# Layer 1's queries at the border between the layers: eighteen tiles as nine pairs in seven quadrant products, and the last block's two tiles beside its keys

## The chip, the cores and the metric

The kernel runs on one core of a Trainium2 chip. The metric is the device time of one execution in microseconds. Five engines take part, each with its own in-order stream of instructions: PE (TensorE, matrix products), DVE (VectorE), ACT (ScalarE), POOL (GpSimd) and SP (SyncE, which here only issues transfers). ACT and POOL issue transfers too, and an issue stands in its engine's stream like any other instruction.

## The reference

Two layers of a graph transformer over 2,708 tokens of width 512, with eight heads of width 64, a feed-forward of width 2,048, and a sparse adjacency (about 3 entries in 1,000):

```python
mask = adj.astype(jnp.float32) + jnp.eye(n, dtype=jnp.float32)
q = (h @ Wq.T + bq).reshape(n, N_HEADS, D_K)
k = (h @ Wk.T + bk).reshape(n, N_HEADS, D_K)
v = (h @ Wv.T + bv).reshape(n, N_HEADS, D_K)
scores = jnp.einsum('nhd,mhd->hnm', q, k) / jnp.sqrt(jnp.float32(D_K))
scores = jnp.where(mask[None, :, :] == 0, jnp.float32(-1000000000.0), scores)
attn = jax.nn.softmax(scores, axis=-1)
ctx = jnp.einsum('hnm,mhd->nhd', attn, v).reshape(n, D_MODEL)
attn_out = ctx @ Wo.T + bo
h1 = _layer_norm(h + attn_out, ln1_g, ln1_b)
ff = jax.nn.relu(h1 @ W1.T + b1) @ W2.T + b2
h2 = _layer_norm(h1 + ff, ln2_g, ln2_b)
```

The output of layer 0 is the input of layer 1. All arithmetic is in float32.

## The kernel before

The tokens are 22 tiles of 128, the last of 20. The neighbours of each token are found first, as lists. Attention then works tile by tile on gathered rows: for each chunk of neighbours POOL gathers one row of keys and values per token (L1119, `kv_d` to `kv`), DVE multiplies the keys with the tile's queries and sums by head (L1156, L1162), ACT takes the exponential and weighs the values (L1175, L1182), and DVE adds them up (L1195). A tile ends with DVE's reciprocal (L1218) and eight scalings on ACT (`cx`, L1226). PE has no part in that; it does the projections and the feed-forward.

The feed-forward takes two tiles at a time, a block. The eleven blocks run in the order (20,19), (18,17), (8,9), (7,10), (6,11), (5,12), (4,13), (3,14), (2,15), (1,16), (21,0), and `order` is that list laid flat. `blocks[0]` of layer 1 is thus (20,19), and the last block of layer 0 is (21,0). A block has 16 steps `f`, after each of which `advance(credit)` draws a few attention steps from the generator `attend`, for the tiles of the next block; `until(g)` draws until tile `g` is attended. In most blocks the two tiles are multiplied by `W1` and `W2` in quadrants, seven products for eight (the *forms* are the sums and differences of the weights' quadrants that this needs; DVE makes them with `form_apart`, L1694 to L1697, and they are stored in `form_d`).

The order of the work is written out by hand. Each engine executes its instructions in the order in which the code writes them, so a line that is written earlier stands earlier in each queue that it uses, and an instruction that waits holds up what is written behind it on its engine. Buffers come from pools with a fixed number for each tag: `row` has 3 (queries before their store, residuals `xb`), `kv` 5 (the gathers' ring), `acc` 2, `cx` 3, `cT` 3, `h` 4, `hT` 1. A write to such a buffer waits until the last use of its former content has ended, a store included.

Between the layers, in the stage called the border here:

- After each block of layer 0, `keys_values` turns the two tiles (`zT`), computes their layer 1 keys and values on PE, and stores them. It also stores `zT` in `zT_d`. For the last block (21,0) this stands behind everything else, because layer 1's attention can begin only when all keys are there.
- `query(g, zT)` computes one tile's queries: four products of 128x512 on PE (L626), one DVE row from PSUM that scales by 1/8 and adds the bias (L1468, the *eviction*), and a store to `q_d`, which is issued one tile later (`kept`, L1479).
- Two tiles' queries lie beside the last keys, fourteen beside the first attention steps, and four around the first two attended tiles, 20 and 19. The two of block (21,0) are computed in block 0's feed-forward of layer 1 (`asking`), and later blocks ask nothing more. Their `zT` come back from `zT_d`: eight loaded in the last block of layer 0 (`preloaded`, in the places of `acc`, `cx` and `h`), two with `two` (in `hT`), the others with `queries` (in `cT`).
- When tile 20 and tile 19 are attended, `attended` turns them, projects them (`o`), adds the residual and normalises: DVE makes the variance (`va`, L1279), POOL its inverse root (`rd`, L1281), DVE scales. `turned` then turns the result, and block 0 begins (L1596).

Of the kernel before, what the change touches and what calls it, by code (L numbers as in the profile page):

```python
# [18 lines left out]
P = 128  # L19
# [21 lines left out]
KVB = 5  # L41
# [446 lines left out]
def by_edges(ctx: ExitStack, tc: tile.TileContext, x, xT, adj, layers, out, redo):  # L488
# [144 lines left out]
    def plus_rest(to, o, r, scale=None):  # L633
        for part in rest(o, r):
            if scale is None:
                nc.vector.tensor_tensor(to, part, to, ALU.add)
            else:
                nc.vector.scalar_tensor_tensor(to, part, scale, to, ALU.mult, ALU.add)

# [718 lines left out]
    class Layer:  # L1358
        def __init__(self, n, w):
            self.n, self.w, self.w1, self.w2, self.due = n, w, [], [], None  # L1360
            self.stages = []
            self.apart, self.other = True, False
# [65 lines left out]
        def preloaded(self, tiles, temp):  # L1428

            places = []  # L1430
            for _ in range(2):
                both = at.tile([P, SLOTS, DM], F32, tag="acc", name="zTs", bufs=2)
                places += [both[:, i] for i in range(SLOTS)]
            places += [at.tile([P, DM], F32, tag="cx", name="zTs", bufs=CXB) for _ in range(CXB)]
            places.append(temp())
            places = [place.rearrange("p (c t) -> p c t", c=NC) for place in places]
            for g, place in zip(tiles, places):
                nc.sync.dma_start(out=place, in_=zT_d[self.n][g])
            return list(zip(tiles, places))

        def two(self, tiles):

            both = dn.tile([P, 2, NC, P], F32, tag="hT", name="zTs", bufs=1)
            for i, g in enumerate(tiles):
                nc.sync.dma_start(out=both[:, i], in_=zT_d[self.n][g])
            return both

        def queries(self, tiles):

            zTs = []  # L1450
            for i in range(len(tiles) + 1):
                while len(zTs) < min(i + 3, len(tiles)):
                    zT = dn.tile([P, NC, P], F32, tag="cT", name="zT", bufs=3)
                    nc.sync.dma_start(out=zT, in_=zT_d[self.n][tiles[len(zTs)]])
                    zTs.append(zT)
                yield
                if i < len(tiles):
                    self.query(tiles[i], zTs[i])
            self.kept()
            yield  # L1460

        def query(self, g, zT):
# [3 lines left out]
            q = project(lambda c: zT[:, c, :r], r, self.wq, "q", self.other and self.apart)  # L1466
# [788 lines left out]
```

## Time and profile before

| | |
|---|---|
| median of 3 runs | 1817.35 us (1817.26 to 1817.72) |
| profiled execution, its own time | 1817.08 us |
| its span | 1815.1 us |
| PE busy | 1791.5 us (99%) |
| DVE busy | 1463.3 us (81%) |
| ACT busy | 1001.1 us (55%) |
| POOL busy | 855.4 us (47%) |
| last keys of layer 1 beside two queries | 1052.4 to 1070.6 us |
| fourteen queries beside the first attention steps | 1070.6 to 1121.3 us |
| first two attended tiles and four queries | 1121.3 to 1143.7 us |
| block 0's feed-forward, up to the next block's second projection | 1143.7 to 1185.4 us |

Times in the trace count from the span's start. A row of a timeline gives the start, the busy time, the engine, the line and the operation, with "output<-input" by the program's names; "x8" means that eight like instructions are drawn together, and a bracket names what the engine waited for before it. A row of waits gives the waiting instruction, what released it, the sum in microseconds, the number of waits and the longest. A row of the groups by line ends with the busy time and the mean of one instruction in nanoseconds. A row of the transfers ends with the median time from issue to landing. A row of the windows gives the stretch, its length, then for PE, PE's weight loads, DVE, ACT and POOL the busy time and the number of instructions, then the granted clock, the busy share of the DMA engines and GB/s.

### The profile page before, as it was taken

Reading aid. Unit: us, or ns where it says so; the run is one execution under the profiler, and the core shown is the slowest. Engines: PE = TensorE matmul, PEld = TensorE weight load, DVE = VectorE, ACT = ScalarE, POOL = GpSimd, SP = SyncE. Lnnn points to the kernel's source line nnn. Section 1 sums busy time; section 2 is a strip of 40 time slices with the busy share of each in tenths; the row PEclk is TensorE's granted clock in tenths of the full one; section 3 lists DMA queues with packets and bytes.
Section 4 is the critical chain, followed back from the end, with each engine's and each line's share of the span. In section 5 each row is a group of like instructions: output and inputs, shape, how many; then the busy total and the mean of one; then the engine's idle time right before and its main releaser. Section 6 shows DMA issues by size and latency. Waiting matters only on the chain. (4 is left out here: it accounts for less than half of the span.)

```text
span 1815.1 us, 23887 instructions
## 1 busy us (share of the span) xinstructions
PE 1791.5 (99%) x6839; PEld 1214.6 (67%) x6839; DVE 1463.3 (81%) x2599; ACT 1001.1 (55%) x3397; POOL 855.4 (47%) x830
## 2 busy tenths in 40 slices
PE   9999999999999999999999999999999999999997
PEld 4444456666777867777677644666666888788786
DVE  4987778988989889799896267988888899989933
ACT  5771436645555555555653104677776677767631
POOL 3333755534454544454540132556665665655312
PEclk9999999999999999999999999999999999999999
DMA  9997987757676675666752777967867787877531
GB/s 335 369 344 252 374 284 245 230 181 241 203 238 220 203 259 192 208 220 202 241 194 73 242 285 272 319 193 256 279 186 263 243 264 237 293 225 234 173 94 36
DMA packets 186728, 426.74 MB, mean 235 GB/s; under 512 B 20550, under 2 KB 83898, under 8 KB 186584
## 3 DMA queue, kind: packets, MB, share of 16 engines
q0 software_dynamic: 76992, 264.49, 44.0%
q1 hardware_dynamic: 99434, 139.01, 22.5%
q10 hardware_dynamic: 10158, 21.61, 3.1%
q8 instruction: 56, 0.92, 0.2%
q14 instruction: 88, 0.72, 0.1%
HBM read 357.13 MB, written 57.11 MB: 228 GB/s over the span
## 5 line engine op out<-in xcount | busy, mean ns | idle before, releaser
L1119 POOL DMA_INDIRECT kv<-kv_d,listed x420 | 526.0, 1252 | 307.2 <-DVE acc L1195 145.8
L1780 PE MATMUL pf<-hT,w 128*128 128x256 f32 x1792 | 407.2, 379 | 2.1 <-ACT ft L1791 2.1
L1780 PEld LDWEIGHTS pf<-hT,w 128*128 128x128 f32 x1792 | 339.2, 190 | 59.2 <-issue 11.0
L1182 ACT ACTIVATE kv<-kv,p 128x64 f32<-128x64 f32 x1232 | 311.0, 335 | 5.0
L1156 DVE TENSOR_TENSOR kv<-kv,q 128x1024 f32<-128x1024 f32 (+1 forms) x222 | 257.1, 1158 | 14.1 <-DMA q<-q_d,ident_i 10.9
L1162 DVE TENSOR_REDUCE sc<-kv 128x16 f32<-128x1024 f32 (+1 forms) x222 | 258.0, 1162 | 7.6
L1195 DVE TENSOR_TENSOR acc<-acc,kv 128x1024 f32<-128x1024 f32 (+2 forms) x178 | 205.6, 1155 | 49.6 <-ACT kv L1182 36.9
L1596 PEld LDWEIGHTS pf<-hT,w 128*128 128x128 f32 x1024 | 178.5, 190 | 55.3 <-issue 34.6
L1596 PE MATMUL pf<-hT,w 128*128 128x256 f32 (+1 forms) x1024 | 214.6, 357 | 0.1
L1791 ACT ACTIVATE ft<-pf,b 128x256 f32<-128x256 f32 x168 | 78.1, 466 | 214.1 <-PE pf L1780 211.4
L1569 PE MATMUL a<-w,ft 128*128 128x512 f32 x416 | 194.6, 592 | 0.0
L1175 ACT ACTIVATE p<-sc,listed 128x8 f32<-128x8 f32 x420 | 103.6, 295 | 127.9 <-DVE sc L1162 116.5
L1281 POOL TENSOR_TENSOR rd<-va,mhalf 128x1 f32<-128x1 f32 (+1 forms) x48 | 43.8, 913 | 230.8 <-DVE va L1279 230.7
L626 PE MATMUL o<-wo,cT 128*128 128x512 f32 x336 | 151.0, 593 | 0.3 <-ACT cT L1354 0.3
L1188 DVE TENSOR_TENSOR kv<-kv,p 128x512 f32<-128x512 f32 (+1 forms) x178 | 123.6, 694 | 4.8 <-ACT p L1175 4.5
L1569 PEld LDWEIGHTS a<-w,ft 128*128 128x128 f32 x416 | 77.7, 190 | 57.5 <-issue 52.0
L626 PEld LDWEIGHTS o<-wo,cT 128*128 128x128 f32 x336 | 63.4, 190 | 69.3 <-issue 59.6
L1331 POOL TENSOR_SCALAR va<-sq 128x1 f32<-128x1 f32 (+1 forms) x40 | 17.2, 429 | 188.4 <-ACT xb L1324 101.9
L751 DVE MAX8 tops<-code 128x8 f32<-128x247 f32 (+2 forms) x242 | 78.8, 400 | 28.0 <-ACT code L746 27.9
L1226 ACT ACTIVATE cx<-acc,su 128x64 f32<-128x64 f32 (+1 forms) x352 | 88.2, 333 | 11.2 <-DVE su L1218 6.2
L1182 ACT ACTIVATE acc<-kv,p 128x64 f32<-128x64 f32 (+1 forms) x352 | 88.8, 335 | 1.4
L746 ACT ACTIVATE code<-aj 128x1354 bf16<-128x1354 int32 (+1 forms) x44 | 73.5, 1724 | 23.7 <-POOL aj L740 19.0
(258 smaller groups left out, 2793.8 us busy)
## 6 DMA issues: line engine op xcount, KB each, us to landing
forms<-form_d SPq DMA_DIRECT2D x294, 128.0 KB, 3.8
aj<-in_adj SPq DMA_DIRECT2D x42, 677.0 KB, 6.3
kv_d<-kvs ACTq DMA_DIRECT2D x21, 512.0 KB, 7.4
h<-ln_b POOLq DMA_DIRECT2D x41, 256.0 KB, 7.0
xg<-in_xT SPq DMA_DIRECT2D x19, 512.0 KB, 8.0
w<-in_W SPq DMA_DIRECT2D x16, 512.0 KB, 6.4
kv<-kv_d,listed POOLq DMA_INDIRECT x420, 6.5
zT_d<-zT SPq DMA_DIRECT2D x22, 256.0 KB, 5.3
```

Source lines behind the costliest of these rows:

```text
L626: nc.tensor.matmul(o[:r], xs(c), wm[:, c, :], start=(c == 0), stop=(c == NC - 1))
L1119: return nc.gpsimd.indirect_dma_start(out=to, out_offset=None, in_=table[:, :], in_offset=bass.IndirectOffsetOnAxis(ap=s, axis=0), bounds_ ...
L1156: nc.vector.tensor_tensor(kv[:r, :c, :DM], kv[:r, :c, :DM], self.q[:r].unsqueeze(1).to_broadcast([r, c, DM]), ALU.mult,)
L1162: nc.vector.tensor_reduce(self.sc[:r, s0 : s0 + c, :], kv[:r, :c, :DM].rearrange("p s (h d) -> p s h d", d=DK), AX.X, ALU.add,)
L1175: nc.scalar.activation(p[:r, s, :], self.sc[:r, s, :], AF.Exp, bias=minus[:r, g, s : s + 1])
L1182: nc.scalar.activation(to[:, i, hd], kv[:r, i, DM + h * DK : DM + (h + 1) * DK], AF.Copy, scale=p[:r, s0 + i, h : h + 1],)
L1188: nc.vector.tensor_tensor(to[:, 0, :].rearrange("p (h d) -> p h d", d=DK), kv[:r, 0, DM:].rearrange("p (h d) -> p h d", d=DK), p[:r, s0, : ...
L1195: nc.vector.tensor_tensor(self.acc[:r, :c, :], self.acc[:r, :c, :], kv[:r, :c, DM:], ALU.add)
L1226: nc.scalar.activation(cx[:r, hd], self.acc[:r, 0, hd], AF.Copy, scale=self.su[:r, h : h + 1])
L1569: nc.tensor.matmul(a[:r, cols], fts[f][:, c0 : c0 + r], self.w2[f // 2][:, f % 2, cols], start=(f == 0), stop=(f == NFC - 1),)
L1596: nc.tensor.matmul(pf[:, :w], self.w1[f // 2][:, c, f % 2 * P : f % 2 * P + P], hT[:, c, :w], start=(c == 0), stop=(c == NC - 1),)
L1780: nc.tensor.matmul(pf[:, :W], self.w1[j][:, c, f % 2 * P : f % 2 * P + P], hT[:, c, :], start=(c == 0), stop=(c == NC - 1),)
```

## The change

Eighteen of the twenty tiles whose queries are made at the border, `order[2:20]`, are now taken in nine pairs. A pair (A, B) is 256 tokens by 512 features; the features and `Wq` are cut in halves, and the four quadrants of the result come from seven products where they took eight (`Seven`): three products of a quadrant with a sum of tokens, and four others, each of two matrix products of 128x256. Four of the products (`first`) fill two PSUM banks, three (`second`) one and a half. `half` is called twice for a pair: first it takes up a pair, writes the next pair's sums (`summed`), the four first products, the pair before's two stores (`kept`) and six DVE rows (`begun`); then the three second products and two DVE rows (`ended`). `begun` and `ended` replace two evictions, and read PSUM in each row.

The four sums of tokens of a pair are made on POOL (`token_sums`), the forms of `Wq` on DVE: three of 128x512 at the border (`form_queries`), and one in place in `wq` (`form_first`, L1541 in the new numbering). Since the direct forms need `Wq` as it was, the first pair's tiles, `order[0:2]`, are computed as before. The scale of 1/8 is now put on `Wq` itself, by four ACT rows in the last block of layer 0. A pair holds two `row` buffers of the three until both stores have ended.

The loads of `zT` are laid elsewhere: eight tiles go to two buffers of the gathers' ring `kv`, two to `cx`, pairs of later tiles to `hT`, `cT` and `cx`, and `h`; two `kv` buffers are thus held until their pairs are done. The two tiles of the last block, 21 and 0, are asked directly in `keys_values`, behind their values and from the `zT` that is there, instead of in block 0 of layer 1; these two `zT` are no longer stored. The number of attention steps between the queries is changed with the number of calls.

The diff, cut:

```diff
+    def token_sums(a, b, to, by):
+
+        a11, a12, a21, a22 = a[:, :2, :], a[:, 2:, :], b[:, :2, :], b[:, 2:, :]
+        s1, s2, s3, s4 = to
+        by.tensor_tensor(s1, a21, a22, ALU.add)
+        by.tensor_tensor(s2, s1, a11, ALU.subtract)
+        by.tensor_tensor(s3, a11, a21, ALU.subtract)
+        by.tensor_tensor(s4, a12, s2, ALU.subtract)
...
+    class Seven:
+
+
+        def __init__(self, a, b, sums, w, forms, banks):
+            s1, s2, s3, s4 = sums
+            t1, t2, t3, t4 = forms
+            L, R = slice(0, W2), slice(W2, DM)
+            self.c0, self.c1, self.a0, self.a1 = banks
...
+            self.first = (
+                (self.c0[:, L], a[:, :2, :], w[:, :2, L]),
+                (self.c0[:, R], s2, t2),
+                (self.c1[:, L], s1, t1),
+                (self.c1[:, R], s3, t3),
+            )
+            self.second = (
+                (self.a0[:, L], a[:, 2:, :], w[:, 2:, L]),
+                (self.a0[:, R], s4, w[:, 2:, R]),
+                (self.a1[:, L], b[:, 2:, :], t4),
...
+        def begun(self, q, bias, more, wide=None):
+
+            L, R = slice(0, W2), slice(W2, DM)
+            nc.vector.tensor_tensor(q[0], self.c0[:, L], bias[:, L], ALU.add)
+            nc.vector.tensor_tensor(q[3], self.c0[:, R], q[0], ALU.add)
+            nc.vector.tensor_tensor(self.c1[:, L], self.c1[:, L], more, ALU.add)
+            if wide is None:
+                nc.vector.tensor_tensor(q[2], self.c1[:, R], q[3], ALU.add)
+                nc.vector.tensor_tensor(q[1], self.c1[:, L], q[3], ALU.add)
...
+            nc.vector.tensor_tensor(q[3], self.c1[:, L], q[2], ALU.add)
+
+        def ended(self, first, q2):
+            nc.vector.tensor_tensor(first, self.a0, first, ALU.add)
+            nc.vector.tensor_tensor(q2, self.a1[:, :W2], q2, ALU.add)
...
-            nc.vector.scalar_tensor_tensor(
-                qs[:r], q[:r], DK**-0.5, self.bq[:r], ALU.mult, ALU.add
-            )
-            plus_rest(qs[:r], q, r, DK**-0.5)
+            nc.vector.tensor_tensor(qs[:r], q[:r], self.bq[:r], ALU.add)
+            plus_rest(qs[:r], q, r)
             self.kept()
-            self.due = (g, qs)
+            self.due = [(g, qs)]
...
+        def form_queries(self):
+
+            w = self.wq
+            b11, b12, b21, b22 = w[:, :2, :W2], w[:, :2, W2:], w[:, 2:, :W2], w[:, 2:, W2:]
+            t3, t2, t4 = [
+                rows.tile([P, DM], F32, tag=tag, name="forms").rearrange("p (c n) -> p c n", c=2)
+                for tag in ("bo", "ln2_g", "e2")
+            ]
+            nc.vector.tensor_tensor(t3, b22, b12, ALU.subtract)
+            nc.vector.tensor_tensor(t2, t3, b11, ALU.add)
+            nc.vector.tensor_tensor(t4, b21, t2, ALU.subtract)
+            self.forms = b12, t2, t3, t4
...
+        def form_first(self):
+
+            w = self.wq
+            nc.vector.tensor_tensor(w[:, :2, W2:], w[:, :2, W2:], w[:, :2, :W2], ALU.subtract)
+            self.more = rows.tile([P, DM], F32, tag="bk", name="more")[:, :W2]
+            nc.gpsimd.tensor_tensor(self.more, self.bq[:, W2:], self.bq[:, :W2], ALU.subtract)
...
+            zA, zB = self.units[0][1]
+            token_sums(zA, zB, self.next_sums, nc.gpsimd)
...
+        def half(self, late=False):
+
+            def begun():
+                qs = [dn.tile([P, DM], F32, tag="row", name="qs", bufs=3) for _ in range(2)]
+                quarters = [t[:, i * W2 : (i + 1) * W2] for t in qs for i in range(2)]
+                one.begun(quarters, self.bq, self.more)
+                return qs
...
+                tiles, (zA, zB) = self.units.pop(0)
+                sums, even = self.next_sums, self.asked_units % 2 == 0
+                self.summed()
...
+                one = Seven(zA, zB, sums, self.wq, self.forms, banks)
+                one.products(one.first)
+                self.kept()
+                self.one = one, tiles, None if late else begun()
+                return
+            one, tiles, qs = self.one
+            qs = qs or begun()
+            one.products(one.second)
+            one.ended(qs[0], qs[1][:, :W2])
+            self.due = list(zip(tiles, qs))
+            self.one = None
...
+                if asking:
+                    asking(g, zT)
...
             for j in (5, 6):
-                now.query(*pool.pop(0))
+                now.half()
                 now.form_apart(j)
             next(ahead)
-            both = now.two(order[8:10])
-            pool += [(g, both[:, i]) for i, g in enumerate(order[8:10])]
-            next(streamed)
             now.stores = nc.scalar
-            while pool:
-                if len(pool) < 5:
+            for i in range(6):
+                if i > 1:
                     advance(0.65)
-                now.query(*pool.pop(0))
-            for i, _ in enumerate(streamed):
-                if i == 1:
-                    both = now.two(order[16:18])
+                now.half()
+            now.loaded(order[16:18], hTs())
+            for i in range(6):
+                now.half()
                 if i == 4:
                     now.stores = nc.sync
                 if len(got) < 2 or i < 3:
                     advance(0.65)
+            now.kept()
             until(blocks[0][0])
             early[n] = now.attended(blocks[0], got, None, True)
             next(early[n])
-            now.query(order[16], both[:, 0])
+            now.loaded(order[18 : 2 * AHEAD], last_places)
+            now.half(True)
             until(blocks[0][1])
             next(early[n])
             for _ in blocks[0]:
                 next(early[n])
-            streamed = now.queries(order[18 : 2 * AHEAD])
-            next(streamed)
-            now.query(order[17], both[:, 1])
+            now.half()
             advance(0.6)
-            next(streamed)
+            now.half()
             advance(0.6)
             *_, hs = early[n]
             early[n] = hs, now.turned(blocks[0], hs)
-            asking = now.queries(blocks[AHEAD])
-            next(asking)
-            finish(streamed)
-            now.apart = False
+            now.half()
+            now.kept()
             now.load_w2(NFC // 2 - 1)
...
-                        pool += nxt.preloaded(order[:8], temp)
+                        for i in (0, 4):
+                            both = at.tile([P, SLOTS, 2 * DM], F32, tag="kv", name="zTs", bufs=KVB)
+                            both = both.rearrange("p s (i w) -> p (s i) w", w=DM)
+                            nxt.loaded(order[i : i + 4], [both[:, k] for k in range(4)])
+                    if f == 8:
+                        cxs = [
+                            at.tile([P, DM], F32, tag="cx", name="zTs", bufs=CXB) for _ in range(CXB)
+                        ]
+                        nxt.loaded(order[8:10], cxs[:2])
...
-            nxt.wq = now.wq
-            for _ in range(2):
-                nxt.query(*pool.pop(0))
-                if len(pool) % 2:
-                    next(behind)
+            nxt.loaded(order[10:12], hTs())
+            (one, other), zTs = nxt.units.pop(0)
+            nxt.query(one, zTs[0])
+            next(behind)
+            nxt.form_queries()
+            nxt.query(other, zTs[1])
             nxt.kept()
             for g in order[:2]:
                 own[g] = asked(n + 1, g)
             finish(behind)
             behind = None
+            nxt.summed()
+            nxt.kept()
+            cTs = [dn.tile([P, NC, P], F32, tag="cT", name="zTs", bufs=3) for _ in range(3)]
+            cTs = [t.rearrange("p c t -> p (c t)") for t in cTs]
+            nxt.loaded(order[12:14], cTs[:2])
+            nxt.loaded(order[14:16], [cTs[2], cxs[2]])
+            last_places = [dn.tile([P, DM], F32, tag="h", name="zTs", bufs=4) for _ in range(2)]
             nxt.staged()
             for j in (3, 4):
                 nxt.form_apart(j)
+            nxt.form_first()
             now = nxt
```

On DVE, at the border, ahead of the first queries of the next stage (rows with `qs` are queries' evictions, `kvs` keys and values, `forms` weight forms). Before:

```order
L636 TENSOR_TENSOR kvs<-k,kvs 20x512 x3
L636 TENSOR_TENSOR kvs<-v,kvs 20x512 x3
L1881 TENSOR_TENSOR kvs<-k,bk 128x512
L1694 TENSOR_TENSOR forms<-w_8251 128x256
L1695 TENSOR_TENSOR forms<-w_8251 128x256
L1696 TENSOR_TENSOR forms<-w_8251,forms 128x256
L1697 TENSOR_TENSOR forms<-w_8251,forms 128x256
L1694 TENSOR_TENSOR forms<-w_8280 128x256
L1695 TENSOR_TENSOR forms<-w_8280 128x256
L1696 TENSOR_TENSOR forms<-w_8280,forms 128x256
L1697 TENSOR_TENSOR forms<-w_8280,forms 128x256
L1468 SCALAR_TENSOR_TENSOR qs<-q,bq 128x512
```

Now:

```order
L1991 TENSOR_TENSOR kvs<-k,bk 128x512
L1514 TENSOR_TENSOR qs<-q,bq 128x512
L1804 TENSOR_TENSOR forms<-w_8252 128x256
L1805 TENSOR_TENSOR forms<-w_8252 128x256
L1806 TENSOR_TENSOR forms<-w_8252,forms 128x256
L1807 TENSOR_TENSOR forms<-w_8252,forms 128x256
L1804 TENSOR_TENSOR forms<-w_8283 128x256
L1805 TENSOR_TENSOR forms<-w_8283 128x256
L1806 TENSOR_TENSOR forms<-w_8283,forms 128x256
L1807 TENSOR_TENSOR forms<-w_8283,forms 128x256
L1541 TENSOR_TENSOR wq<-wq 128x2x256
L690 TENSOR_TENSOR qs<-q_8519,bq 128x256
```

Behind the eight form rows stood the next tile's eviction; now the row on `wq` stands there, which PE's third product of the first pair needs, and behind it that pair's `begun` (L690 on).

On POOL, in the query stage (`kv<-kv_d` is a gather, `sums` the sums of tokens, `rd` the inverse root in the first two tiles' norm). Before, from the last keys' scatter on:

```order
L1869 MEMSET zT 128x512
L1082 DMA kv_d_112<-kvs,ident_i 2708x1024 x2
L1119 DMA kv<-kv_d_112,listed 128x1024 x17
L1281 TENSOR_TENSOR rd<-va,mhalf 128x1 x2
L1119 DMA kv<-kv_d_112,listed 128x1024 x7
L1343 DMA h<-ln_b 128x512 x2
```

Now, a part of the stage's gathers:

```order
L1188 DMA kv<-kv_d_112,listed 128x1024 x7
L655 TENSOR_TENSOR sums<-zTs 128x256
L656 TENSOR_TENSOR sums<-sums,zTs 128x256
L657 TENSOR_TENSOR sums<-zTs 128x256
L658 TENSOR_TENSOR sums<-zTs,sums 128x256
L1188 DMA kv<-kv_d_112,listed 128x1024 x2
L655 TENSOR_TENSOR sums<-zTs 128x256
L656 TENSOR_TENSOR sums<-sums,zTs 128x256
L657 TENSOR_TENSOR sums<-zTs 128x256
L658 TENSOR_TENSOR sums<-zTs,sums 128x256
L1188 DMA kv<-kv_d_112,listed 128x1024 x4
```

and the end of the stage, with the last pair's sums:

```order
L655 TENSOR_TENSOR sums<-zTs 128x256
L656 TENSOR_TENSOR sums<-sums,zTs 128x256
L657 TENSOR_TENSOR sums<-zTs 128x256
L658 TENSOR_TENSOR sums<-zTs,sums 128x256
L1350 TENSOR_TENSOR rd<-va,mhalf 128x1 x2
L1188 DMA kv<-kv_d_112,listed 128x1024 x7
L1412 DMA h<-ln_b 128x512 x2
```

Where seventeen gathers stood in one row, sums of tokens stand between them, and both `rd` now have the last pair's four sums ahead of them.

On ACT, between the first and the second attended tile (`cx` are the scalings that end a tile, `q_d<-qs` the queries' stores). Before:

```order
L1226 ACTIVATE cx<-acc,su 128x64 x8
L1479 DMA q_d_114<-qs 128x512 x2
L1175 ACTIVATE p<-sc,listed 128x8 x2
L1182 ACTIVATE kv<-kv,p 128x64 x8
L1226 ACTIVATE cx<-acc,su 128x64 x8
L1479 DMA q_d_114<-qs 128x512
L1354 ACTIVATE cT<-tp,bv 128x128 x8
```

Now:

```order
L1295 ACTIVATE cx<-acc,su 128x64 x8
L1522 DMA q_d_114<-qs 128x512 x2
L1244 ACTIVATE p<-sc,listed 128x8 x2
L1251 ACTIVATE kv<-kv,p 128x64 x8
L1295 ACTIVATE cx<-acc,su 128x64 x8
L1522 DMA q_d_114<-qs 128x512 x2
L1423 ACTIVATE cT<-tp,bv 128x128 x8
```

The stores of a tile are now the two of a pair, and they stand behind the same scalings.

More of the change, by code (lines that the diff above doesn't have):

```diff
@@ L1426, in load_next, with loaded @@
             self.nbo = self.unsettled[-1][0]
[L1428 to L1460 removed]
+        def loaded(self, tiles, places):
+            zTs = []
+            for g, place in zip(tiles, places):
+                zT = place.rearrange("p (c t) -> p c t", c=NC)
+                nc.sync.dma_start(out=zT, in_=zT_d[self.n][g])
+                zTs.append(zT)
+            for i in range(0, len(zTs), 2):
+                self.units.append((tiles[i : i + 2], zTs[i : i + 2]))
         def query(self, g, zT):
@@ L2032, in by_edges @@
         if n > 0:
-            streamed = now.queries(order[10:16])
             got = {}
```

75 lines of the change are left out of this document (59 added, 16 removed).

## The prediction

> **What bounds the kernel now.** I read the page's first part, then PE's waits, then a table of windows by stage, then the timelines of the border between the layers. The whole span first:
>
> ```profile
> PE 1791.5 (99%) x6839; PEld 1214.6 (67%) x6839; DVE 1463.3 (81%) x2599; ACT 1001.1 (55%) x3397; POOL 855.4 (47%) x830
> ```
>
> PE is busy 99% of the span, so products saved are time saved, if nothing else becomes late. Where that could happen the windows show: the border (last keys), the queries of layer 1 beside the first attention steps, the first two attended tiles, and block 0's feed-forward up to its second projection.
>
> ```profile
> 1052.40:1070.60 18.20, 17.32 (x57) 7.05 (x56) 15.76 (x30) 2.37 (x9) 3.31 (x4) 1.00 0.69 242
> 1070.60:1121.30 50.70, 48.54 (x113) 21.06 (x112) 35.45 (x54) 17.35 (x68) 18.45 (x18) 1.00 0.84 309
> 1121.30:1143.70 22.40, 22.40 (x66) 10.79 (x65) 13.80 (x21) 6.69 (x26) 5.60 (x5) 1.00 0.52 172
> 1143.70:1185.40 41.70, 41.40 (x154) 26.87 (x152) 39.50 (x50) 28.71 (x112) 24.25 (x20) 1.00 0.99 346
> ```
>
> The third column is PE, the fifth DVE. In the query stage DVE works 35.45 of 50.70 us, in block 0's first part 39.50 of 41.70: two engines lie close together here, and PE's few waits of layer 1 stand in just these stages:
>
> ```profile
> PE q L626 <- DVE acc L1195: 1.6, 1, 1.6
> PE q L626 <- DMA zT<-zT_d: 0.5, 1, 0.5
> PE o L626 <- ACT cT L1354: 0.3, 1, 0.3
> ...
> 1103.87 8.36 DMA q_d<-qs
> ...
> 1112.92 0.69 DVE qs L1468
> ...
> 1116.59 1.24 DVE acc L1195
> 1117.83 3.67 PE q L626 x8
> ```
>
> The last four rows are the chain of waits inside the query stage: a query's store that took 8.36 us held its row buffer, DVE stood before the next eviction, the attention rows behind it came late, and so did PE. Three `row` buffers and DVE's order already decide here.
>
> **PE's part.** The stage's rows on PE:
>
> ```profile
> 1070.63 17.33 PE L626 MATMUL q<-wq,zTs 128*128 128x512 f32 x40
> ...
> 1117.82 3.67 PE L626 MATMUL q<-wq,zT 128*128 128x512 f32 x8 [1.61 <-DVE acc L1195]
> 1121.33 0.60 PE L1349 MATMUL tp<-ident,cx 128*128 128x128 f32 x4
> ...
> 1125.64 7.03 PE L626 MATMUL o<-wo,cT 128*128 128x512 f32 x16
> ...
> 1143.69 7.07 PE L1596 MATMUL pf<-hT,w 128*128 128x256 f32 x32
> ...
> 1152.40 1.05 PE L621 MATMUL q<-wq,zT 128*20 128x512 f32 x8
> ...
> 1167.27 3.60 PE L626 MATMUL q<-wq,zT 128*128 128x512 f32 x8
> ...
> 960.97 3.62 PE L1780 MATMUL pf<-hT,w 128*128 128x256 f32 x16
> 964.42 0.59 PE L1769 MATMUL a<-forms 128*128 128x256 f32 x2
> ```
>
> Five tiles take 17.17 us from start to start, 3.43 each. A 128x256 product, two records, takes (964.42 - 960.97)/8 = 0.431. A pair was 6.87 and becomes 14 products, 6.04; nine pairs save 7.5 us. The two moved queries (1.0 and 3.43) leave block 0 and go to the border: nothing in PE's sum, but 4.4 us earlier.
>
> **DVE's part.** Prices:
>
> ```profile
> 1068.01 0.41 DVE L1694 TENSOR_TENSOR forms<-w 128x256 f32<-128x256 f32 x1
> 1068.34 0.42 DVE L1695 TENSOR_TENSOR forms<-w 128x256 f32<-128x256 f32 x1
> 1068.79 0.43 DVE L1696 TENSOR_TENSOR forms<-w,forms 128x256 f32<-128x256 f32 x1
> ...
> 1070.84 0.42 DVE L1697 TENSOR_TENSOR forms<-w,forms 128x256 f32<-128x256 f32 x1
> ...
> 1101.58 1.88 DVE L1468 SCALAR_TENSOR_TENSOR qs<-q,bq 128x512 f32<-128x512 f32 x3
> ...
> 1118.83 0.20 DVE L1218 RECIPROCAL su<-su 128x8 f32<-128x8 f32 x1
> ...
> 1161.43 2.13 DVE L638 SCALAR_TENSOR_TENSOR qs<-q,qs 20x512 f32<-20x512 f32 x3
> ...
> L1824 DVE TENSOR_TENSOR u<-c,u 128x256 f32<-128x256 f32 x14 | 5.9, 425 | 1.5
> ```
>
> A 128x256 row costs 0.33 us, 0.46 where it needs the row before it; from PSUM it is no dearer (425 ns). A 128x512 eviction costs 0.60. `begun` is six rows, three of them dependent, 2.4; `ended` 0.60 + 0.33. A pair costs DVE 3.3 us where two evictions cost 1.2: 19 us more in all, against PE's 7.5 saved.
>
> At the border DVE also gets three 128x512 rows (2.0) and the 20-row query's four (2.8), with 2.4 idle in that window; I take 0.8 of wait for PE (from 0, if all hides, to 2.4). Then v(0) leaves PE at 1070.6 + 1.0 + 0.8 = 1072.4 and q(0) at 1075.9. Behind q(0)'s eviction (0.6) stand eight forms (1068.01 to 1071.26, 3.2), which before ran while PE did v(0), and only then the row that makes `wq`'s quadrant (128x512, 0.6): 1080.3. PE's third product waits for it from 1077.6, 2.7 us.
>
> From there to the reciprocal of the second attended tile, which ended at 1119.0, DVE has: its attention rows (the stage's 35.45, less 13 evictions at 0.63 and nine forms at 0.36: 24), eight forms 3.2, six pairs 19.8. That is 47, so 1127.3 if DVE never waits.
>
> It does wait. `begun`'s second row writes a buffer from which the pair before is stored. The store's price:
>
> ```profile
> q_d<-qs SPq DMA_DIRECT2D x4, 256.0 KB, 2.7
> ...
> zT<-zT_d SPq DMA_DIRECT2D x8, 256.0 KB, 5.7
> ...
> 1119.13 0.35 ACT L1226 ACTIVATE cx<-acc,su 128x64 f32<-128x64 f32 x1 [2.57 <-DVE su L1218]
> 1119.36 0.33 ACTq L1479 DMA_DIRECT2D q_d<-qs  x1
> 1119.38 1.76 ACT L1226 ACTIVATE cx<-acc,su 128x64 f32<-128x64 f32 x7
> ```
>
> Issue 0.33 and landing from 2.7 (quiet) to 8.36 (the chain). Between the pairs DVE's own rows cover it for 2.2, 5.7, 3.9, 0.5 and 4.3 us, but at the second and fifth the store stands on ACT behind eight scalings (2 us), or sixteen, that themselves wait for DVE. With landings of 3.3 that leaves about 1.4 + 3.3 + 0 + 3.1 + 1.2, some 9 us; 7 with 2.7, 30 with 8.36 each time. I take 9, near the quiet rows, since slower attention also thins the gathers. The reciprocal ends at T = 1136.3, 17.3 late.
>
> **Behind it.** Sixth pair's stores stand on ACT behind the eight `cx` rows (1119.13 to 1121.14, 2.0): the seventh pair's `begun` resumes at T + 5.5 and its `ended` is done at T + 8.4. Only then can SP pass that pair's two stores, two residual loads and the last pair's two zT loads (six issues, 0.4 each), which land 5.7 to 7.2 later: T + 17. Pool:
>
> ```profile
> zTs<-zT_d SPq DMA_DIRECT2D x11, 256.0 KB, 7.2
> ...
> L964 POOL TENSOR_TENSOR kvs<-kvs,bk 128x512 f32<-128x512 f32 x20 | 25.4, 1270 | 50.7 <-ACT kvs L962 39.8 <-issue 4.8 <-DMA aj<-in_adj 3.9
> ...
> 1076.15 1.06 POOL L1119 DMA_INDIRECT kv<-kv_d,listed  x1 [3.42 <-issue]
> 1077.52 1.00 POOL L1119 DMA_INDIRECT kv<-kv_d,listed  x1 [0.30 <-issue]
> ...
> 1131.25 0.94 POOL L1281 TENSOR_TENSOR rd<-va,mhalf 128x1 f32<-128x1 f32 x1 [21.79 <-DVE va L1279]
> ```
>
> Half of 1.27 is 0.65 for a 128x256 sum, 2.6 a pair; the two `rd` rows of the norms are queued behind the last pair's sums, so the first ends at T + 20.5. The norms (scale 0.5, 2.5, `rd` 0.95, scale 0.5) end at T + 25, the eighth pair's ten-odd rows at T + 28.3, one attention chunk (2.4) and the ninth's `begun` (2.4) at T + 33; its last products and the turned tiles put block 0 at T + 35. Before it was 1143.7 - 1119.0 = 24.7. Start of block 0: 17.3 + 10.3 = 27.6 late.
>
> Pool also makes PE wait inside the stage: the gather that needs the pair buffer of the third pair stands ahead of the fourth pair's sums, two gathers (2.6) and two sums (1.3) less one product (0.9), 3 us, and similar later. Those waits lie beside DVE's chain and are not added.
>
> In block 0 PE loses 4.4 us of work, DVE 3.4 of evictions; but the gathers for its next tiles, issued from 1094 on before, now stand behind `rd`, at T + 26, and DVE has no slack there. I take 6 us of new wait at the projection that waited 0.3 (from 0 to 9). Sum: 27.6 - 4.4 + 6 = +29.2. The profiled execution took 1817.08 with a span of 1815.1, the runs' median is 1817.35: 1846.5.
>
> **The rivals.** *PE decides after all* (other side). If stores and sums were always there before they are needed, PE would save 7.5 and its old 2.2 of waits, and pay 2.7 and 0.8: -6, 1811. For it: 99%. Against it: PE would want the second tile at 1075.9 + 7 x 6.04 + 0.4 + 3.45 = 1122, its reciprocal 2 us (the `cx` rows) earlier, at 1120, and DVE's rows alone end at 1127.3. It decides only if a pair costs DVE 7.3/6 less, 2.1 us.
>
> *Only DVE's rows count*, every store covered: T = 1127.3, block 0 at T + 24.7, so +8.3, less 4.4, plus 2 for the late keys: +5.9, 1823. Against it: the 8.36.
>
> *Stores as in the chain*, or longer: landings of 6 us instead of 3.3 at five hand-overs, of which three are bare: +8 to +13 more, 1855 to 1860; with 8.36 over 1862.
>
> *Pool and DVE block each other.* If a sum on Pool and a DVE row with two SBUF inputs cannot run together, the 24 sums before T (0.65 each) stop DVE for up to 16 us: +10 at two thirds, 1857. No row here has the two side by side: L964's adds ran beside DVE's search, which has one input.
>
> [...]
>
> **How the numbers follow.** Forecast 0.67, spanning 1829 to 1856; slow stores 0.06 and the lock 0.06, above; DVE's rows alone 0.08, about 1823; PE 0.09, about 1811; both cancelling, no change, 0.04. 0.2% of 1817 (3.6 us) is about what a measurement here tells from nothing. The range 1821 to 1861 leaves out the two lowest cases, 0.13, and the top of the slow ones, 0.03; the forecast's own is 1829 to 1856. Faster 0.09, same 0.04, slower 0.87.
>
> **What would show it.** The second tile's reciprocal at 1130 to 1145 instead of 1119; DVE idle some 3 us each before three or four of the `begun` second rows, released by `q_d<-qs`; about 5 us there behind the reciprocal; Pool idle long before the last sums, released by a zT load, and `rd` after them; block 0 starting near 1171; PE's waits of layer 1 grown from under 3 to above 25 us, all before 1230. Wrong it would be if block 0 began before 1150, if the `begun` rows never waited for stores, or if a pair took DVE under 2 us.

## The result and the profile after

The changed kernel takes 1845.67 us (median of 4 runs, 1845.2 to 1847.0) against 1817.37 before on the same chip: a ratio of 1.0157 (95% interval 1.0139 to 1.0174), 28.3 us slower. The profiled execution took 1845.3 us with a span of 1843.4, which is 28.3 above the span before, so its trace accounts for the whole loss.

The first part of the page, then the same four stages as before: last keys, query stage, first two attended tiles, block 0 up to the next block's projection (columns as before; the last three are the granted clock, the DMA share and GB/s).

```profile
PE 1794.6 (97%) x6947; PEld 1241.5 (67%) x6947; DVE 1488.0 (81%) x2657; ACT 1003.5 (54%) x3401; POOL 884.5 (48%) x867
```

```profile
1052.00:1072.10 20.10, 18.20 (x65) 7.30 (x64) 18.01 (x30) 2.51 (x9) 3.31 (x4) 1.00 0.68 236
1072.10:1146.10 74.00, 58.02 (x226) 46.77 (x225) 57.74 (x105) 18.27 (x72) 47.27 (x51) 0.88 0.61 203
1146.10:1172.30 26.20, 19.19 (x69) 12.89 (x68) 15.68 (x32) 5.69 (x22) 7.58 (x9) 0.84 0.46 150
1172.30:1213.30 41.00, 37.71 (x138) 25.95 (x136) 38.25 (x48) 28.37 (x111) 23.85 (x20) 0.98 0.96 345
```

The query stage has grown from 50.7 to 74.0 us, the norm stage from 22.4 to 26.2, the last keys from 18.2 to 20.1; block 0 is 0.7 shorter. DVE works 57.74 of the 74.0 us. PE's 58.02 us are more than its work, since part of them ran at a granted clock of 0.50 and 0.51 (last section). PE's waits:

```profile
PE q L683 <- POOL sums L656: 8.5, 3, 4.2
PE q L683 <- DVE wq L1541: 5.7, 1, 5.7
PE q L683 <- DVE qs L703: 4.5, 1, 4.5
PE o L626 <- ACT cT L1423: 3.3, 1, 3.3
...
PE tp L1418 <- DVE qs L703: 2.5, 1, 2.5
```

DVE's timeline, with the places at which it waits, two `begun` second rows (L691) that wait for nothing, and the reciprocal of the second attended tile:

```profile
1076.69 0.95 DVE L1805 TENSOR_TENSOR forms<-w 128x256 f32<-128x256 f32 x1
...
1082.36 0.68 DVE L1541 TENSOR_TENSOR wq<-wq 128x512 f32<-128x512 f32 x1
...
1086.98 0.43 DVE L692 TENSOR_TENSOR q<-q,more 128x256 f32<-128x256 f32 x1 [3.15 <-PE q L683]
...
1094.01 0.42 DVE L691 TENSOR_TENSOR qs<-q,qs 128x256 f32<-128x256 f32 x1 [0.90 <-DMA q_d<-qs]
...
1102.73 0.42 DVE L691 TENSOR_TENSOR qs<-q,qs 128x256 f32<-128x256 f32 x1
...
1118.56 0.42 DVE L690 TENSOR_TENSOR qs<-q,bq 128x256 f32<-128x256 f32 x1 [1.63 <-PE q L683]
1122.23 0.42 DVE L691 TENSOR_TENSOR qs<-q,qs 128x256 f32<-128x256 f32 x1 [3.24 <-DMA q_d<-qs]
...
1134.53 0.42 DVE L691 TENSOR_TENSOR qs<-q,qs 128x256 f32<-128x256 f32 x1
...
1140.86 0.20 DVE L1287 RECIPROCAL su<-su 128x8 f32<-128x8 f32 x1
...
1143.51 0.43 DVE L691 TENSOR_TENSOR qs<-q,qs 128x256 f32<-128x256 f32 x1 [2.15 <-DMA q_d<-qs]
...
1168.39 0.42 DVE L691 TENSOR_TENSOR qs<-q,qs 128x256 f32<-128x256 f32 x1 [2.19 <-DMA q_d<-qs]
```

POOL at the end of the stage, and SP ahead of it (between the stores and the zT loads stand two residual loads):

```profile
1152.92 0.73 POOL L655 TENSOR_TENSOR sums<-zTs 128x256 f32<-128x256 f32 x1 [14.16 <-DMA zTs<-zT_d]
...
1155.77 0.57 POOL L1350 TENSOR_TENSOR rd<-va,mhalf 128x1 f32<-128x1 f32 x1
```

```profile
1146.14 0.80 SPq L1522 DMA_DIRECT2D q_d<-qs  x2
...
1148.67 0.90 SPq L1503 DMA_DIRECT2D zTs<-zT_d  x2
```

The chain stands as it was drawn: DVE to the second reciprocal (1141.06), then the seventh pair's stores on SP, the last pair's zT behind them, POOL's last sums, `rd`, the norms, block 0 at 1172.32.

### The profile page after: what moved, and what is told of

Read it like the earlier page. It is cut to its first block, busy times and chain, and to the rows that moved or that the text cites. A ratio compares the mean times of both kernels' runs of the same rounds, so it can differ in the third digit from the quotient of the medians.

```text
span 1843.4 us, 24216 instructions
## 1 busy us (share of the span) xinstructions
PE 1794.6 (97%) x6947; PEld 1241.5 (67%) x6947; DVE 1488.0 (81%) x2657; ACT 1003.5 (54%) x3401; POOL 884.5 (48%) x867
## 4 chain that ended last, share of the span: by engine, by line
PE 82%; DVE 8%; issue 4%; ACT 2%; DMA 2%; POOL 1%; POOLq 0%; DVEq 0%; ACTq 0%
PE pf L1890 17%; PE pf L1706 9%; PE a L1679 8%; PE k L626 8%; PE v L626 8%; PE c L1879 8%; PE o L626 7%; PE a L1879 6%; PE q L626 4%; PE tp L1418 2%; DVE kv L1225 1%; DVE sc L1231 1%; PE a L1914 1%; PE a L1910 1%; ACT kv L1251 1%
## 5 line engine op out<-in xcount | busy, mean ns | idle before, releaser
L1225 DVE TENSOR_TENSOR kv<-kv,q 128x1024 f32<-128x1024 f32 (+1 forms) x222 | 257.4, 1159 | 12.2 <-DMA q<-q_d,ident_i 10.9
```

The costliest lines, as they stand in the source:

```text
L1225: nc.vector.tensor_tensor(kv[:r, :c, :DM], kv[:r, :c, :DM], self.q[:r].unsqueeze(1).to_broadcast([r, c, DM]), ALU.mult,)
```

## The experiments

Layer 0's part alone differed by up to 5 us between the profiled executions (tile 21's keys began between 1060.2 and 1065.0 us). So beside the medians the table gives two stretches of each profiled execution: from the start of the first product of tile 21's keys (L621, `k`) to block 0's start, and to the end of the span. For the changed kernel there are two such executions; their mean is 782.8, and the kernel before has 754.5. Every other run has one. A gain by the medians is taken from the ratios, against the mean of the change's two, 1.0163; the ratios' intervals are some 3 us to either side, so gains of a few microseconds are not certain to the microsecond.

| run | median us | before beside it | ratio (95%) | keys to block 0 | keys to end |
|---|---|---|---|---|---|
| before | 1817.37 | | | 83.1 | 754.5 |
| the change | 1845.67 | 1817.37 | 1.0157 (1.0139 to 1.0174) | 112.1 | 783.2 |
| the change again | 1849.58 | 1818.24 | 1.0169 (1.0150 to 1.0189) | 111.3 | 782.5 |
| first_early | 1848.59 | 1818.29 | 1.0167 (1.0150 to 1.0184) | 111.3 | 782.8 |
| early_load | 1843.83 | 1818.29 | 1.0137 (1.0120 to 1.0154) | 109.8 | 783.4 |
| bias_stored | 1838.64 | 1818.29 | 1.0115 (1.0098 to 1.0132) | 104.5 | 774.4 |
| no_sums | 1844.28 | 1818.29 | 1.0141 (1.0124 to 1.0158) | 108.2 | 779.4 |
| more_rows | 1843.31 | 1818.24 | 1.0136 (1.0118 to 1.0154) | 108.7 | 779.4 |
| three_fixes | 1840.52 | 1818.41 | 1.0127 (1.0110 to 1.0145) | 106.1 | 776.7 |
| all_four | 1828.15 | 1818.41 | 1.0056 (1.0039 to 1.0073) | 93.3 | 763.5 |
| all_four_two_rows | 1813.77 | 1818.41 | 0.9977 (0.9967 to 0.9986) | 79.9 | 749.0 |
| two_moved | 1818.72 | 1818.41 | 0.9998 (0.9988 to 1.0008) | 85.0 | 755.3 |
| before_sums | 1825.38 | 1818.24 | 1.0033 (1.0022 to 1.0044) | 89.5 | 761.2 |

**First the row on wq.** Order alone:

```diff
+            nxt.form_first()
             for j in (3, 4):
                 nxt.form_apart(j)
-            nxt.form_first()
```

> The row that makes wq's quadrant and the small row on POOL are put ahead of the eight form rows of the border. If DVE's chain sets the end (my theory), PE's wait of 5.7 us at the first pair's third product falls below 1 us, DVE's idle 3.15 us before that pair's third row goes, the second tile's reciprocal ends some 3 us earlier than 1141, and the time is about 1842.5 us. If the wait only moves on to the next store or the next sums, PE's wait goes all the same, but the time stays within 1 us of 1845.7.

The wait for the wq row went, and nothing was gained: 782.8 to the end, as without it. Its PE and DVE waits show where it moved:

```profile
PE q L683 <- POOL sums L656: 11.9, 4, 4.3
```

```profile
DVE qs L691 <- DMA q_d<-qs: 12.2, 5, 4.3
```

Waits for sums grew from 8.5 to 11.9 us, waits for stores from 8.5 to 12.2. By the medians, too, nothing was gained (1.0167). My 3 us were wrong, the other reading held: a wait in front of the next one in the same chain is no price of its own.

**The last pair's zT early.**

```diff
+            nxt.loaded(order[18 : 2 * AHEAD], last_places)
+            last_pair = nxt.units.pop()
             nxt.staged()
...
-            now.loaded(order[18 : 2 * AHEAD], last_places)
+            now.units.append(last_pair)
```

> The last pair's two zT loads are issued at the border, where their places are already held, instead of behind the seventh pair's stores and the residuals. If POOL's last sums hold up the norm (my theory), POOL's idle 14.2 us before them goes, the first rd row begins as soon as DVE has made va, 3.6 us earlier, and the time falls by 3 to 4 us, to about 1842. If DVE or the stores of the eighth pair set block 0's start anyway, it falls by less than 1 us.

POOL's 14 us wait went, `rd` now waits for `va` alone, and block 0 began 2.0 us earlier than the mean of the change:

```profile
1157.40 1.01 POOL L1350 TENSOR_TENSOR rd<-va,mhalf 128x1 f32<-128x1 f32 x1 [9.62 <-DVE va L1348]
```

```profile
1172.86 2.07 PE L683 MATMUL q<-forms,zTs 128*128 128x256 f32 x4 [5.31 <-DVE qs L703]
1174.72 8.91 PE L1706 MATMUL pf<-hT,w 128*128 128x256 f32 x32
...
1216.10 5.32 PE L626 MATMUL o<-wo,cT 128*128 128x512 f32 x8 [2.77 <-ACT cT L1423]
```

To the end nothing is left of it in this execution: block 0's first 32 products took 8.91 us (7.97 in the change, 7.07 before) and the projection 5.32 (3.70). PE ran slowly there, as below: the four records just ahead of block 0 took 2.07 us, others of their kind 1.03. But this execution was the slowest of the run's four by 6 us (1850.24; the others 1842.22 to 1844.27), and by the medians the gain is 4.7 us, a little above the 3 to 4 expected. The mechanism is shown; its worth for the total is between nothing and 5 us and not settled.

**Stores without a hold on the row buffers.** Layer 1's queries are left out here of what attention reads.

```diff
-                self.stores.dma_start(out=q_d[self.n][g * P : g * P + r, :], in_=qs[:r])
+                self.stores.dma_start(out=q_d[self.n][g * P : g * P + r, :], in_=self.bq[:r])
```

> Each query's store takes its bytes from the bias row, so that no row buffer waits for a store; layer 1's queries are thereby left out of what attention reads, the stores and all other work stay. If the store waits count in full (my theory), DVE's four idle times released by a store (0.9, 3.2, 2.2 and 2.2 us) go and the time falls by about 8 us, to 1838. If PE's products or POOL's sums are next in line, it falls by 0 to 3 us.

It gained 8.4 us (782.8 to 774.4; 8.7 by the medians): the four waits of 0.9, 3.2, 2.2 and 2.2 are 8.5, and none of them is left. The full reading held.

**Without the sums of tokens.** Four of a pair's seven products take a sum of tokens, three a quadrant as it is; here all seven take quadrants.

```diff
-            token_sums(zA, zB, self.next_sums, nc.gpsimd)
+            self.next_sums = [zB[:, :2, :], zA[:, :2, :], zB[:, 2:, :], zA[:, 2:, :]]
```

> The 36 sums of tokens on POOL are left out; the products take quadrants of the tiles themselves, so the queries are other numbers, in the same number of products. If the sums cost by POOL's order and by slowing DVE's rows beside them (my theory), the eight form rows go from 6.0 back to 3.2 us, PE's 8.5 us of waits for sums go, the rd wait of 3.6 us goes, and the time falls by 9 to 12 us, to about 1835. If only the last sums count, it falls by 3 to 4 us, to 1842, and if DVE's own rows decide it all, by less than 2 us.

The rows behaved as I said, the total did not. The form rows, by line, of the change (1072.0 to 1083.1) and of this run (1072 to 1090):

```profile
L1805 DVE TENSOR_TENSOR forms<-w 128x256 f32<-128x256 f32 x2 | 1.9, 944 | 0.0
L1806 DVE TENSOR_TENSOR forms<-w,forms 128x256 f32<-128x256 f32 x2 | 1.7, 836 | 0.1
```

```profile
L1805 DVE TENSOR_TENSOR forms<-w 128x256 f32<-128x256 f32 x3 | 1.3, 419 | 0.0
L1806 DVE TENSOR_TENSOR forms<-w,forms 128x256 f32<-128x256 f32 x3 | 1.3, 425 | 0.1
```

The mean fell to half, PE's wait for wq from 5.7 to 2.8, and the waits for sums went. But DVE's waits for stores took the room:

```profile
DVE qs L691 <- DMA q_d<-qs: 12.9, 6, 4.3
```

12.9 us for 8.5. The gain was 3.4 us (4.0 by the medians) where I had said 9 to 12. That is the number of the reading in which only the last sums count; the trace does not decide for it, since the earlier waits for sums went as well and the stores' waits grew.

**Places for three pairs' queries**, with nothing left out.

```diff
+            nxt.more_rows = [dn.tile([P, DM], F32, tag="h", name="qs", bufs=4) for _ in range(2)]
...
+                self.begun_pairs = getattr(self, "begun_pairs", -1) + 1
+                if self.begun_pairs in (1, 3, 5):
+                    qs = self.more_rows
+                else:
+                    qs = [dn.tile([P, DM], F32, tag="row", name="qs", bufs=3) for _ in range(2)]
-                qs = [dn.tile([P, DM], F32, tag="row", name="qs", bufs=3) for _ in range(2)]
```

> The changed kernel with one thing changed: the second, fourth and sixth pair take two free h buffers for their queries instead of row buffers; nothing is left out. If the stores' waits are the cause (my theory), the two before the second tile's reciprocal (0.9 and 3.2 us) and the one behind it (2.2) go and the time is 4 to 6 us below the changed kernel. If the three fixes gained by the order and the loads, it is within 2 us of it.

The store waits fell from 8.5 to 2.3 us (the last one). By the profiles the gain is 3.4 us (782.8 to 779.4), by the medians beside the change on this chip 6.3 (1849.58 to 1843.31); the expected 4 to 6 lies between. So the stores count in the kernel as it computes, too.

**The three fixes together.**

> Nothing is left out here: wq's row goes ahead of the forms, the last pair's zT is loaded at the border, and the second, fourth and sixth pair take two free h buffers for their queries instead of row buffers, so that five of the eight hand-overs wait for no store. If the stores are the largest single cause (my theory), DVE's waits for q_d stores fall from 8.5 us to under 5, and the time is 7 to 11 us below the changed kernel, about 1837. If sums and products take the stores' place, it is 2 to 4 us below.

6.1 us by the profiles (782.8 to 776.7), 6.5 by the medians: under the 7 to 11 expected, above the 2 to 4 of the rival. DVE's waits for stores fell to 2.7 us, as expected. What is left in PE's waits is sums and DVE's rows:

```profile
PE q L683 <- POOL sums L656: 11.4, 4, 5.1
PE q L683 <- DVE qs L703: 8.8, 2, 5.6
```

**All four at once**, and then with two DVE rows a pair.

> Four edits on the changed kernel at once: wq's row ahead of the forms, the last pair's zT loaded at the border, the stores taken from the bias row, the sums of tokens left out. What stays of the change is PE's nine pairs, DVE's eight rows a pair and the two moved tiles. If DVE's own rows are the rest of the loss (my theory), the time is 6 us above the kernel before (4 to 11), block 0 begins 80 us or less behind q(0)'s eviction where the change has 96.6, and PE's waits of layer 1 are under 12 us. If something else that is still there sets the end (gathers that wait for the two kv buffers, PE's slower clock), it stays 15 us or more above.

```diff
-            nc.vector.tensor_tensor(q[0], self.c0[:, L], bias[:, L], ALU.add)
...
+            nc.vector.tensor_tensor(wide, self.c0, bias, ALU.add)
...
-            nc.vector.tensor_tensor(first, self.a0, first, ALU.add)
-            nc.vector.tensor_tensor(q2, self.a1[:, :W2], q2, ALU.add)
+            nc.vector.tensor_tensor(first, self.a0, self.bias, ALU.add)
```

> As the run before, and begun and ended are one 128x512 row each instead of eight rows; the parts c1 and a1 are computed on PE and not added, so layer 1's queries are left out of the result altogether. If DVE's price of a pair is what eats PE's gain (my theory), the time is 4 to 8 us below the kernel before, about PE's own saving of 7.5. If the gathers or the places of the tiles decide, it stays above the kernel before.

The first is 10 us above the kernel before (7 to 13; 9.0 by the profiles), of which 6 had been put down to DVE's rows. Its block 0 begins 77.8 us behind q(0)'s eviction, and PE's waits behind the last keys are 12.2 us, a little over the 12 expected. By the profiles the four edits gained 0.0, -0.6, 8.4 and 3.4 us singly, 11 in all, and 19.3 together. By the medians it is -0.7, 4.7, 8.7 and 4.0, 16.7 in all, and 19.5 together. Whether the four together gain more than their sum is therefore not shown. What the traces do show is that a wait removed alone comes back in part as another one: behind the row on `wq` and behind the sums the waits for stores grew, from 8.5 to 12.2 and 12.9.

The second is 4.2 us below the kernel before (2.5 to 6.0; 5.5 by the profiles): most of PE's saving of 7.5 is there, and the six DVE rows a pair that are left out cost 14.5 us (763.5 to 749.0; 14.4 by the medians), 1.6 a pair. So what this run still has of the change, the gathers' two `kv` buffers, the other places and the two moved tiles, does not set the loss. Behind the last keys PE waits in it only for these:

```profile
PE o L626 <- ACT cT L1410: 2.4, 1, 2.4
...
PE pf L1693 <- ACT hT L1410: 1.4, 1, 1.4
```

**The two moved tiles alone.**

```diff
+                if asking:
+                    asking(g, zT)
+                else:
+                    nc.sync.dma_start(out=zT_d[n][g], in_=zT)
...
+                behind = now.keys_values(block, zs, None if more else nxt.query)
```

> The kernel before with one part of the change alone: tiles 21 and 0 are asked beside their keys, nothing is paired. If the pairs are the whole loss (my theory), the time is within 2 us of the kernel before. If the later last key (4.4 us of PE ahead of or beside it, 3.4 us of DVE) starts attention later and nothing makes it up, it is 2 to 5 us above.

0.9998 (0.9988 to 1.0008): no difference. The later keys cost 1.9 us up to block 0 (85.0 for 83.1), and block 0, without its two queries, gives about half of it back in this execution (755.3 to the end for 754.5).

**Sums on POOL in the kernel before**, two for each tile, read by nobody.

> The kernel before with 36 sums of 128x256 on POOL, two for each of tiles order[2:20], into places that nothing reads. If POOL's sums cost by themselves, by slowing DVE's rows beside them and by standing ahead of gathers (my theory), DVE's 128x256 and 128x512 rows beside them take up to twice as long, and the time is 2 to 6 us above the kernel before. If they cost only where a product waits for them, it is within 1.5 us of it.

6.0 us by the ratio (4.0 to 8.0), 6.7 by the profiles, but for another reason than mine:

```profile
PE q L626 <- DMA zT<-zT_d: 6.6, 3, 2.7
```

```profile
SPq L1454 <- POOL spare L1475: 15.3, 4, 6.4
```

POOL's late sums held the `cT` places, so SP issued the next tiles' zT late (L1454 are those loads, `spare` the sums). DVE's rows did slow down as I had said: a form row beside sums took 0.93 us, the ones behind it 0.41 to 0.43, and the rows with two SBUF inputs together took some 4 us more in this stage than in the kernel before. But PE waited for none of them, and what they cost alone the run does not tell. Here work on an in-order POOL is paid through what it keeps.

## Why the prediction was right

The forecast was 1846.5 and the time 1845.67; the sum of its terms, +29.2, compares with +28.3. The sum is nearer than its terms, and that part is luck: T came 4.8 us later than forecast, the way from T to block 0 was 3.7 shorter and block 0 1.9 shorter.

| step | forecast | measured |
|---|---|---|
| v(0) leaves PE (before: 1070.6) | 1072.4 | 1072.1 |
| the row on wq ends | 1080.3 | 1083.0 |
| DVE's work from there to the second reciprocal | 47 | 49.1 |
| DVE's idle in it | 9 | 8.9 |
| second reciprocal, T | 1136.3 | 1141.06 |
| from T to block 0 (before: 24.7) | 35 | 31.3 |
| block 0 to the end | +1.6 | -0.3 |

*PE's nine pairs.* A product of two records took 0.43 us, as costed, and PE's gain exists: the run with two DVE rows takes 5.5 us less than the kernel before. It could not be had at DVE's price.

*DVE's price of a pair.* The eight rows are 0.41 to 0.43 each and 0.68 for the wide one, as taken from the form and eviction rows. This is the largest single term, 14.5 us by the two combined runs. The rival in which DVE's rows alone count gave +5.9; its 1127.3 holds the late keys already, so without counting their 2 us a second time it gave +3.9. The run that comes nearest to it gave 10 (7 to 13), since even without stores and sums PE still waits and then runs slowly: its block 0 begins with

```profile
1156.70 8.86 PE L1706 MATMUL pf<-hT,w 128*128 128x256 f32 x32 [0.33 <-ACT hT L1423]
```

8.86 us for 7.07.

*The row on wq behind eight forms* came 2.7 us later than forecast: six of the eight form rows took 0.83 to 0.95 us beside POOL's sums where the other two took 0.41 and 0.42, and in the run without sums all are short, as the by-line rows above show. That is the effect of the fourth rival, which I had given 0.06 (“the lock”) and +10. It is there and smaller: the forms lose 2.8 us, and the attention rows with two SBUF inputs 2.1 more in the stage, by the groups of the kernel before (1075 to 1144) and of the change (1072 to 1174):

```profile
L1156 DVE TENSOR_TENSOR kv<-kv,q 128x1024 f32<-128x1024 f32 x7 | 8.5, 1218 | 2.7 <-DMA kv<-kv_d,listed 2.7
L1195 DVE TENSOR_TENSOR acc<-acc,kv 128x1024 f32<-128x1024 f32 x3 | 3.7, 1224 | 1.8 <-ACT kv L1182 1.6
L1188 DVE TENSOR_TENSOR kv<-kv,p 128x512 f32<-128x512 f32 x4 | 2.7, 683 | 0.1
```

```profile
L1225 DVE TENSOR_TENSOR kv<-kv,q 128x1024 f32<-128x1024 f32 x7 | 8.8, 1258 | 0.0
...
L1264 DVE TENSOR_TENSOR acc<-acc,kv 128x1024 f32<-128x1024 f32 x3 | 4.7, 1562 | 0.3
L691 DVE TENSOR_TENSOR qs<-q,qs 128x256 f32<-128x256 f32 x9 | 3.8, 425 | 8.6 <-DMA q_d<-qs 8.5
...
L1257 DVE TENSOR_TENSOR kv<-kv,p 128x512 f32<-128x512 f32 x4 | 3.5, 868 | 0.0
```

The busy times differ by 0.3, 1.0 and 0.8 us, which is as much as DVE's work up to T was more than forecast, 49.1 for 47. It goes both ways: sums of 0.72 us took 0.79 to 0.94 beside the form rows and up to 1.72 beside the wide attention rows. The pair's own rows, which take one input from PSUM, kept 425 ns, also those that ran beside sums (1094.35 to 1095.60). So the sums and the DVE rows with two SBUF inputs both took longer side by side; that the two cannot run together, as the rival had it, no run shows. Without the sums the slow rows went, but the total fell by 3.4 us only.

*The stores.* 9 us of idle were forecast before T, and 8.9 were there, but only 4.1 of them (0.90 and 3.24) were stores; 3.15 and 1.63 were waits for PE's own products. The prediction had left PE's waits for sums “beside DVE's chain”, and had no wait of DVE for the first pair's products behind the row on `wq`; but PE was late and, behind its waits, slow. The stores were forecast, hand-over by hand-over, at 1.4, 3.3, 0, 3.1 and 1.2 us and measured 0.90, 0, 0, 3.24 and 0; the two that came to nothing are the second and the fifth, where the store was to stand on ACT behind scalings. These are the two steps that failed inside a right sum, and that they cancel is luck. Taken over the whole border the stores gained most of the single edits: 8.5 us idle, 8.4 gained.

*Behind T* the forecast was 3.7 us too long. It had the sixth pair's stores stand 2 us on ACT behind the eight `cx` rows. They did not:

```profile
1141.16 0.35 ACT L1295 ACTIVATE cx<-acc,su 128x64 f32<-128x64 f32 x1 [7.01 <-DVE su L1287]
1141.39 0.33 ACTq L1522 DMA_DIRECT2D q_d<-qs  x1
```

Written behind eight scalings, the first issue came 0.23 us after the first of them had begun; at the first tile it came even before the first had:

```profile
1128.99 0.33 ACTq L1522 DMA_DIRECT2D q_d<-qs  x1
1129.15 0.57 ACT L1295 ACTIVATE cx<-acc,su 128x64 f32<-128x64 f32 x2
```

The rows of before quoted in the prediction (the issue at 1119.36, the first scaling at 1119.13) had said the same. `begun` resumed at T + 2.5, not T + 5.5. The order of the rest held: POOL waited 14.16 us for the last zT, which it had at T + 11.9 instead of T + 17, and `rd` stood behind the sums.

*Block 0.* The 4.4 us of queries went, the projection waits 3.29 us where it waited 0.30, and the first 32 products take 7.97 for 7.07: -0.5 together, -0.3 measured. I had taken 6 us of new wait; it was 3.0.

*The other rivals.* “PE decides” fell with 25 us and more of PE's waits. Slow stores came singly: the landing was 2.1 us in the median for the twelve issued on ACT, but the one behind the wait of 3.24 us took 5.50:

```profile
q_d<-qs ACTq DMA_DIRECT2D x12, 256.0 KB, 2.1
...
1116.63 5.50 DMA q_d<-qs
```

At the other hand-overs before T DVE waited 0.90 us or nothing, so this rival's three to five long waits did not come.

What stays open: how the 18 us between the change and the run with four edits divide between stores, sums and the last pair's load, since each takes the other's place in part; what the slow rows beside POOL cost by themselves; and what PE's slow clock costs, which no run takes away by itself.

## What to carry to other kernels

Saved products are worth something only if the engine that adds the parts together has room: here seven products for eight save PE 0.83 us a pair and cost DVE 2.1, in a stage where DVE had been busy for 35 of 50.7 us and was now busy for 58 of 74. Price a wait by the chain it stands in, not by its length: the fix of a 5.7 us wait gave nothing, since the waits behind it grew. Three places for pairs that hold two until they are stored were too few: with two more, taken by three of the pairs, DVE's waits for stores fell from 8.5 to 2.3 us. And a sum on an in-order POOL should not stand ahead of a row that the critical chain needs: here DVE waited 3.65 us for `rd` behind the last pair's sums.

## What was unexpected of the hardware

**PE at half its clock behind waits.** Windows of the changed kernel, a wait of PE and the products behind it, the products behind a second wait, and those behind a third:

```profile
1078.84:1083.09 4.25, 0.00 (x0) 0.00 (x0) 4.18 (x7) 0.00 (x0) 3.86 (x5) 0.87 0.54 194
1083.09:1088.37 5.28, 5.28 (x12) 4.21 (x13) 2.03 (x6) 0.00 (x0) 3.99 (x4) 0.50 0.83 261
...
1107.59:1112.80 5.21, 5.21 (x13) 4.20 (x14) 5.18 (x6) 0.00 (x0) 4.75 (x4) 0.51 0.53 188
...
1164.03:1165.94 1.91, 1.91 (x5) 1.01 (x3) 1.88 (x3) 0.03 (x1) 0.00 (x0) 0.50 0.74 228
```

After 5.65 us without work the granted clock was 0.50 for the next 5.3 us, and 0.51 for 5.2 us behind a wait of 4.15; behind a wait of 0.98 it was 1.00. Between these the length alone does not decide: it was 0.50 in the last window too, where PE had waited 2.50 us with transposes on both sides, but the wait of 3.29 us ahead of the next block's projection left it at 1.00 (3.70 us, as in the kernel before). So the waits with a slow stretch behind them were paid a second time, and DVE, which waited for PE, waited longer: its 3.15 us at the first pair are two products of four records that took 3.6 us where 1.7 would do, at the 0.86 us of those behind them.

**An issue on ACT did not wait for the ends of the scalings written ahead of it**: it left 0.23 us after the first of eight had begun, where waiting for all eight would have taken 2 us, and at the first tile 0.16 us before the first had begun.
